# The last products of two token blocks made together: two levels of Strassen's scheme in place of one, with the outer sums of the weights made in DRAM

## The chip, the core and the metric

The kernel runs on one core of one Trainium2 chip. The metric is the device time of one execution in microseconds; lower is better.

## The reference

The reference is one decoder layer on `x`, 1024 tokens (2 sequences of 512) of 1024 features, all in float32. Three parts follow each other, and after each the input of the part is added and a layer norm is taken:

```python
# 1 attention over features: per token, q is [32, 32 heads], k and v are [32, 8 heads] repeated 4 times
scores = einsum('bsdh,bseh->bsde', q, k) / sqrt(32)
out    = einsum('bsde,bseh->bsdh', softmax(scores), v)
# 2 product with the context, both sides rounded to 8 bits
matmul(fake_quant(x, 8/255, 128), fake_quant(ctx, 8/255, 128))
# 3 feed-forward with a routed part
h      = relu(x @ up_w) ** 2                            # 1024 -> 2048
routed = (x @ fc1_w) @ expert_w * sum(top2(x @ gate_w))  # 1024 -> 512 -> 512
layernorm(h @ down_w + routed @ fc2_w) * gamma + beta
```

Part 1 has no product between tokens: it is elementwise work of 32 x 32 sums for each token. Part 3 holds most of the arithmetic. Its last step is a product of 2560 features (2048 of `h`, 512 of the routed part) with 2560 x 1024 weights.

## The kernel before

Tokens lie in eight tiles of 128, and two tiles make a block, so there are four blocks. The text calls a tile "a token" where it says token 2, token 3 and so on, as the code's names do (`s_3`, `xc_4`).

The work has two tracks. **The tokens' path** (`token_path`, L636) takes the tiles one after another. `scores` (L428) multiplies q and k on DVE (L435) and sums over heads (L441) in four pieces. `exponentials` (L448) takes the row maximum (L450) and subtracts it (L451) on DVE, and then takes exp on ACT (L454). `attend` (L458) multiplies with v (L468), sums (L474), divides (L479) and adds to the residual `xc` (L489). `normalise_aside` (L309) makes the layer norm: ACT makes the sum (L317), the squares (L322), the variance (L324), POOL the power (L326), ACT the shift (L330) and the result (L331). `cross` (L575) rounds on ACT (L346, L349, L352, L602), transposes with a DMA from ACT's queue (L605), multiplies with the rounded context on PE (L618) and adds to `xc` on DVE (L611, L612, L623). `hand_over` (L683) transposes the tile for the feed-forward (L133, L134) and adds the last norm's beta with an accumulating DMA from POOL's queue (L690). `context_beside` (L510) rounds the second sequence's context beside all this.

**The feed-forward** is PE's track. For blocks 0 and 1 `ffn` (L768) makes 16 products of 128 hidden features (L780, 8 chunks of weights of 1 MB, two PSUM banks `ps_mm` in turn), each taken out by ACT's relu (L798) and square (L799), then 4 products of the routed part taken out by DVE (L809), and then `down` (L983), the last product over 20 pieces of 128 features, accumulated in four PSUM banks (L994). `gate_of` (L723) makes the routing. For blocks 2 and 3 `ffn_pair` (L824) makes the first products of both together by Strassen's scheme in ten steps of 7 products (L881), and then `down_seven` (L1039) makes the last product of one block and then of the other: for each half of the 1024 columns and each group of four pieces, `weight_sums` (L1027) loads 1 MB and makes four sums of weights on DVE, `unit_sums` (L1014) makes four sums of hidden features, and 7 x 2 matmuls of 128 x 128 by 128 x 256 follow (L1080). In all these are 2 blocks x 2 halves x 5 groups x 14 = 280. Seven products stand for the eight of a 2 x 2 product of blocks.

A front stage comes first: queries, keys and values of all eight tiles are made on PE (`project_qk`, `project_v`), those of tiles 2 to 7 go through staging tiles (`new_qkv`, L167) into `qkv_d` in DRAM with accumulating DMAs (`projected`, L179), and `fetch_qkv` (L173) brings them back one tile ahead of their scores from POOL's queue. `expert_w` and `fc2_w` are multiplied there into `e2`, 512 x 1024 in DRAM, so that the routed part has one product fewer later.

The program is written as generators that interleave both tracks. The loop at the end of the kernel advances the tokens' path while the sum of its yielded weights times PACE = 0.7 is below the sum of the feed-forward's. A scheduler then orders each engine's instructions by its own estimates, except where `tc.issue_after` pins one instruction behind another. On the chip each engine takes its queue strictly in that order and waits on semaphores for what it needs. A pool that is opened after another was closed takes over its memory; whoever first writes there waits for the last use of what lay there, DMAs included.

## Time and profile before

| | us |
|---|---|
| median of 3 runs (lowest to highest) | 727.29 (725.45 to 727.51) |
| profiled execution | 725.26 |
| its span in the profile | 723.2 |
| outside the span | 2.06 |
| front stage, to the first scores of token 2 | 0 to 139.4 |
| block 0, to the first of block 1's products | 139.4 to 309.9 |
| block 1, to the pair's first product | 309.9 to 466.2 |
| pair, first products | 466.2 to 588.6 |
| pair, last products | 588.6 to 709.6 |
| tail | 709.6 to 723.2 |

Times in a timeline or a window count from the start of the span. A row of a timeline has the start, the busy time, engine, line and operation, what is written and read, and in brackets how long the engine stood idle before and what ended that. Rows of groups have the busy time, the mean of one in ns, and the idle time before them. The trace counts a float32 matmul as two rows, so 560 rows of L1080 are 280 products of the program.

### The profile page before, as it was taken

To read this page: it belongs to the slowest core of one execution; us is meant where nothing else is said; L and a number is where in the kernel's file an instruction comes from. 1 tells how busy PE (TensorE), PEld (TensorE's weight loads), DVE (VectorE), ACT (ScalarE), POOL (GpSimd) and SP (SyncE) were. 2 spreads that over 40 slices of the span, in tenths; PEclk is the share of its full clock that TensorE was granted. 3 is DMA by queue.
4 is the path that set the end of the run, shared out by engine and by line. 5 is a ranking of instruction groups with operands and counts; after the bars stand their busy time and mean duration, and the time that the engine had idled before them with its cause. 6 is when DMAs were issued, how large, how long until landed. Compare 5 with 4: busy or idle time off the path is not lost. (4 is left out here: it accounts for less than half of the span.)

```text
span 723.2 us, 7274 instructions
## 1 busy us (share of the span) xinstructions
PE 696.0 (96%) x2802; PEld 494.5 (68%) x2812; DVE 545.3 (75%) x619; ACT 239.1 (33%) x389; POOL 63.8 (9%) x96
## 2 busy tenths in 40 slices
PE   6999998999999999999999999999999999999992
PEld 3656653468876444478785444588888888888882
DVE  4799987599999999999899920545545754779736
ACT  2097643222644389138453141212422100000001
POOL 2011211210001020011010000100100000001001
PEclk9999999999999999999999999999999999999996
DMA  8999523695455666456448344522332235556501
GB/s 284 340 296 374 155 39 102 216 293 165 154 163 157 203 230 203 150 162 229 131 147 218 116 157 149 155 78 77 127 105 100 61 116 176 174 174 205 201 1 58
DMA packets 71554, 120.05 MB, mean 166 GB/s; under 512 B 10640, under 2 KB 44944, under 8 KB 71520
## 3 DMA queue, kind: packets, MB, share of 16 engines
q1 hardware_dynamic: 57344, 98.84, 40.4%
q0 software_dynamic: 6496, 18.39, 9.9%
q10 hardware_dynamic: 7680, 2.36, 1.5%
q8 instruction: 22, 0.36, 0.2%
q14 instruction: 12, 0.10, 0.0%
HBM read 106.73 MB, written 11.01 MB: 163 GB/s over the span
## 5 line engine op out<-in xcount | busy, mean ns | idle before, releaser
L994 PE MATMUL pd<-dn,h 128*128 128x512 f32 x320 | 138.7, 592 | 0.0
L780 PE MATMUL pu<-x2T,up 128*128 128x256 f32 x512 | 112.4, 380 | 1.3 <-DMA up<-in_L_ffn_up_w_dram 0.8
L994 PEld LDWEIGHTS pd<-dn,h 128*128 128x128 f32 x320 | 60.5, 190 | 73.2 <-issue 72.7
L780 PEld LDWEIGHTS pu<-x2T,up 128*128 128x128 f32 x512 | 96.8, 190 | 15.6 <-ACT relu L798 1.2
L435 DVE TENSOR_TENSOR pqk<-qk 128x2048 f32<-128x2048 f32 x32 | 72.4, 2282 | 0.0
L441 DVE TENSOR_REDUCE s<-pqk 128x256 f32<-128x2048 f32 x32 | 72.3, 2277 | 0.1
L468 DVE TENSOR_TENSOR pav<-s,v 128x2048 f32<-128x2048 f32 x32 | 72.2, 2277 | 0.0
L474 DVE TENSOR_REDUCE o<-pav 128x64 f32<-128x2048 f32 x32 | 71.9, 2266 | 0.0
L152 PE MATMUL pqk<-wqkv,xT 128*128 128x512 f32 x128 | 66.1, 616 | 0.8 <-DVE wqkv L233 0.5
L1034 DVE TENSOR_TENSOR tt<-dn 128x1024 f32<-128x1024 f32 x20 | 24.3, 1221 | 24.7 <-DMA dn<-in_L_ffn_down_w_dram 15.5
L157 PEld LDWEIGHTS pv<-wqkv,xT 128*128 128x128 f32 x128 | 24.3, 190 | 24.2 <-issue 22.0
L1080 PE MATMUL ps<-dn,h 128*128 128x256 f32 x160 | 40.4, 379 | 0.0
L1080 PE MATMUL ps<-dn,s 128*128 128x256 f32 x160 | 40.4, 379 | 0.0
L1080 PE MATMUL ps<-tt,h 128*128 128x256 f32 x160 | 40.4, 379 | 0.0
L1092 ACT COPY y<-ps 128x256 f32<-128x256 f32 x4 | 1.5, 372 | 109.9 <-PE ps L1080 109.9
L157 PE MATMUL pv<-wqkv,xT 128*128 128x256 f32 x128 | 35.6, 379 | 0.0
L1080 PEld LDWEIGHTS ps<-dn,s 128*128 128x128 f32 x160 | 30.4, 190 | 4.1
L1080 PEld LDWEIGHTS ps<-tt,h 128*128 128x128 f32 x160 | 30.4, 190 | 4.1
L1080 PEld LDWEIGHTS ps<-dn,h 128*128 128x128 f32 x160 | 30.4, 190 | 4.1
L152 PEld LDWEIGHTS pqk<-wqkv,xT 128*128 128x128 f32 x128 | 24.3, 196 | 12.6 <-issue 5.5
L419 PE MATMUL pe<-fc,exT 128*128 128x512 f32 x64 | 29.9, 619 | 2.5 <-DVE xc L623 2.5
L326 POOL TENSOR_TENSOR rstd<-ve,neg_half 128x1 f32<-128x1 f32 x18 | 14.1, 784 | 200.9 <-ACT ve L324 200.2
(204 smaller groups left out, 1009.5 us busy)
## 6 DMA issues: line engine op xcount, KB each, us to landing
dn<-in_L_ffn_down_w_dram SPq DMA_DIRECT2D x32, 1024.0 KB, 5.1
up<-in_L_ffn_up_w_dram SPq DMA_DIRECT2D x16, 1024.0 KB, 5.5
dn<-e SPq DMA_DIRECT2D x8, 1024.0 KB, 5.0
pair<-in_L_ffn_up_w_dram SPq DMA_DIRECT2D x8, 1024.0 KB, 5.3
fc<-in_L_ffn_fc_w_dram SPq DMA_DIRECT2D x6, 1024.0 KB, 5.9
xs<-in_x_dram SPq DMA_DIRECT2D x8, 512.0 KB, 7.4
wq<-in_L_attn_Wq_dram SPq DMA_DIRECT2D x8, 512.0 KB, 6.1
xc<-in_x_dram SPq DMA_DIRECT2D x8, 512.0 KB, 8.4
```

The costliest lines, as they stand in the source:

```text
L152: projecting[0] = nc.tensor.matmul(pqk, xT[:, k, :], wqkv[k][:, 0 : 2 * DG], start=(k == 0), stop=(k == KE - 1))
L157: nc.tensor.matmul(pv[:, :DG], xT[:, k, :], wqkv[k][:, 2 * DG : 3 * DG], start=(k == 0), stop=(k == KE - 1),)
L326: nc.gpsimd.tensor_tensor(rstd, ve, neg_half, ALU.pow)
L419: expert[0] = nc.tensor.matmul(ps, exT[:, m, ts(l, P)], fc2[m // 2][:, m % 2, ts(n, HALF)], start=(m == 0), stop=(m == NL - 1),)
L435: nc.vector.tensor_tensor(prod.rearrange("p (d e g) -> p d e g", d=DC, g=G), q3[:, ts(c, DC), :].unsqueeze(2).to_broadcast([P, DC, D, G]), ...
L441: nc.vector.tensor_reduce(s[:, ts(c, DC), :].rearrange("p d e -> p (d e)"), prod.rearrange("p (c g) -> p c g", g=G), AX.X, ALU.add,)
L468: nc.vector.tensor_tensor(prod.rearrange("p (d g e) -> p d g e", d=DC, g=G), s[:, ts(c, DC), :].unsqueeze(2).to_broadcast([P, DC, G, D]), ...
L474: nc.vector.tensor_reduce(o[:, ts(c, DC), :].rearrange("p d g -> p (d g)"), prod.rearrange("p (c e) -> p c e", e=D), AX.X, ALU.add,)
L780: lately[0] = nc.tensor.matmul(ps[:, :NB], ws[:, k, wcols], xT[:, k, :], start=(k == 0), stop=(k == KE - 1))
L994: lately[0] = nc.tensor.matmul(pd[i][n], h[kk // 4][:, i, kk % 4, :], w[:, k, ts(n, HALF)], start=(kk == 0), stop=(kk == NK - 1),)
L1034: nc.vector.tensor_tensor(tt[:, 0:2], w[:, 1], w[:, :, 0], ALU.subtract)
L1080: began[m] = lately[0] = nc.tensor.matmul(banks[m], units[jj][m][:, k, :], weights[gg][m][:, k, :], start=begins and not second, stop=(jj ...
```

## The change

Four things are changed.

1. The last products of blocks 2 and 3 are made together by Strassen's scheme on two levels. The outer level splits the two blocks (rows), the halves of each group's 512 features and the halves of the columns; each of its seven products is made by an inner level of seven. There are 49 x 5 matmuls of 128 x 128 by 128 x 256, 245.
2. The outer level's sums of weights don't depend on tokens. `outer_sums` makes them in DRAM: for four of the seven (`OUTER_T`) and each of three chunks of groups, a copy from SP's queue and an accumulating DMA from POOL's queue, each over DRAM alone, 1 MB for the first two chunks and 0.5 MB for the last. They are issued a step at a time beside blocks 0 and 1.
3. `new_h` makes one tile per block instead of five, and the sums of hidden features get tiles of a pool `units` and of `late`. Pool `more` is closed before the pair.
4. The staging tiles of queries, keys and values move from `attp` (where their tags were shared with the sums of hidden features) to `frontp`, which is closed before pools `h`, `ffn`, `sums` and `more` are opened.

The core of the diff:

```diff
     qkv_d = scratch.tile([NT, P, 3 * DG], F32, name="qkv_d")
-    KEPT = NK // 4
+    KEPT = 5
 
     def new_qkv(t, away):
-        pool, bufs = (attp, KEPT) if away else (tokp, 2)
-        qk = pool.tile([P, 2 * DG], F32, tag="s12" if away else "qk", name=f"qk_{t}", bufs=bufs)
-        v = pool.tile([P, G, D], F32, tag="s4" if away else "v", name=f"v_{t}", bufs=bufs)
+        pool, bufs = (frontp, KEPT) if away else (tokp, 2)
+        qk = pool.tile([P, 2 * DG], F32, tag="qk", name=f"qk_{t}", bufs=bufs)
+        v = pool.tile([P, G, D], F32, tag="v", name=f"v_{t}", bufs=bufs)
         return qk, v
 
...
-    def new_h(blk, k):
+    def new_h(blk):
 
         pool, tag = (pools["late"], "h_late") if blk > PAIR else (pools["h"], "h")
-        return pool.tile([P, TB, 4, P], F32, tag=tag, name=f"h_{blk}_{k}", bufs=NK // 4)
+        return pool.tile([P, NG, TB, 4, P], F32, tag=tag, name=f"h_{blk}")
...
-        h = ([], [])
-        sums = []
+        h = [new_h(blk) for blk in blks]
+        outer_steps, outer = outer_units(*h)
+        down = down_pair(outer)
+        next(down)
...
+            if g % 2 == 1:
+                next(outer_steps)
+                if g // 2 + 1 in [hi for _, hi in CHUNKS]:
+                    next(down)
         phase[0] = "down"
-        down_seven(PAIR, h[0], sums, next_block)
-        down_seven(PAIR + 1, h[1], next_sums)
+        next(down, None)
...
-        if blk < PAIR:
+        if blk < NBLK - 1:
             sums = small.tile([P, 1], F32, tag="sum3", name=f"sum3_{blk}_{i}")
             nc.vector.scalar_tensor_tensor(
                 y, y, rstd, xcs_of[blk][i], ALU.mult, ALU.add, accum_out=sums
             )
-            later.append(store_aside(rows, y, sums, f"3_{blk}_{i}", len(later)))
+            aside = store_aside(rows, y, sums, f"3_{blk}_{i}", len(later))
+            if blk < PAIR:
+                later.append(aside)
+            else:
+                for _ in aside:
+                    pass
             return
         nc.vector.scalar_tensor_tensor(y, y, rstd, xcs_of[blk][i], ALU.mult, ALU.add)
-        if blk < NBLK - 1:
-            normalise(y, f"3_{blk}_{i}")
-            nc.gpsimd.dma_start(rows, y)
-            return
 
...
+    CHUNKS = ((0, 2), (2, 4), (4, 5))
 
...
+    OUTER_T = (4, 5, 6, 7)
+    tw = {
+        (m, c): scratch.tile([(hi - lo) * 2 * P, HALF], F32, name=f"tw_{m}_{c}")
+        for m in OUTER_T for c, (lo, hi) in enumerate(CHUNKS)
+    }
+
+    def raw_rows(c, half, n):
+
+        lo, hi = CHUNKS[c]
+        src = down_w if 4 * lo < NI else e2
+        lo, hi = (lo, hi) if 4 * lo < NI else (lo - NI // 4, hi - NI // 4)
+        v = src.rearrange("(j h q) n -> j h q n", h=2, q=2 * P)
+        return v[lo:hi, half, :, ts(n, HALF)]
+
+    def outer_sums():
+
+        for _ in range(12):
+            yield
+        for c, (lo, hi) in enumerate(CHUNKS):
+            b11, b12, b21, b22 = (raw_rows(c, half, n) for half in range(2) for n in range(2))
+            t = {m: tw[m, c].rearrange("(j q) n -> j q n", q=2 * P) for m in OUTER_T}
+            for to, src in ((5, b11), (7, b12), (6, b22), (4, b21)):
+                nc.sync.dma_start(t[to], src)
+                for _ in range(2):
+                    yield
+            for to, src in ((5, b12), (7, b22), (6, t[5]), (4, t[6])):
+                nc.gpsimd.dma_start(t[to], src, accum_op=ALU.add, max_dma_last_dim=4 * HALF)
+                for _ in range(6):
+                    yield
+
+    def outer_units(ha, hb):
+
+        ss = [
+            pools[pool].tile([P, NG, TB, 2, P], F32, tag=f"units_{i}", name=f"units_{i}")
+            for i, pool in enumerate(("units", "units", "late"))
         ]
+        a11, a12, a21, a22 = (h[:, :, :, 2 * k : 2 * k + 2, :] for h in (ha, hb) for k in range(2))
+
+        def steps():
+            for j in range(NG):
+                s1, s2, s4 = (s[:, j] for s in ss)
+                nc.vector.tensor_tensor(s1, a21[:, j], a22[:, j], ALU.subtract)
+                nc.vector.tensor_tensor(s2, s1, a11[:, j], ALU.subtract)
+                nc.vector.tensor_tensor(a21[:, j], a11[:, j], a21[:, j], ALU.subtract)
+                nc.vector.tensor_tensor(s4, a12[:, j], s2, ALU.add)
+                yield
+
+        return steps(), {1: a11, 2: a12, 3: ss[2], 4: a22, 5: ss[0], 6: ss[1], 7: a21}
+
+
+    OUTER = ((1, 0), (5, 1), (6, 0), (7, 1), (3, 0), (2, 1), (4, 0))
+
+    def down_pair(outer):
+        inner_units, inner_weights = {}, {}
+
+        def units_of(o, lo=0, hi=NG):
+
+            m = OUTER[o][0]
+            x = outer[m]
+            a11, a12, a21, a22 = (x[:, :, i, k, :] for i in range(2) for k in range(2))
...
+        def weights_of(o, c):
+
+            m = OUTER[o][0]
+            lo, hi = CHUNKS[c]
+            nj = hi - lo
+            tag = ("wb", "wb", "wa", "wa")[len(inner_weights) % 4]
+            w = wstream.tile([P, nj, 4, QW], F32, tag=tag, name=f"dn_{m}_{c}")
+            if m in OUTER_T:
+                src = tw[m, c].rearrange("(j k r) n -> r j k n", k=2, r=P)
+            else:
+                src = raw_rows(c, int(m != 1), int(m == 3))
+                src = src.rearrange("j (k r) n -> r j k n", r=P)
+            to = w.rearrange("p j (k e) n -> p j k (e n)", k=2)
+            if m in OUTER_T:
+                nc.sync.dma_start(to, src)
+            else:
+                for j in range(nj):
+                    nc.sync.dma_start(to[:, j], src[:, j])
+            tt = pools["sums"].tile([P, 3, nj, QW], F32, tag="tt", name=f"tt_{m}_{c}")
+
+            b12 = w[:, :, 1, :]
+            t1, t3, t4 = tt[:, 0], tt[:, 1], tt[:, 2]
+            nc.vector.tensor_tensor(
+                tt[:, 0:2], w[:, :, 0::3, :].rearrange("p j q n -> p q j n"),
+                b12.unsqueeze(1).to_broadcast([P, 2, nj, QW]), ALU.add,
+            )
+            nc.vector.tensor_tensor(b12, w[:, :, 3, :], t1, ALU.add)
+            nc.vector.tensor_tensor(t4, w[:, :, 2, :], b12, ALU.add)
+            inner_weights[o, c] = {
+                1: w[:, :, 0, :], 2: w[:, :, 2, :], 3: w[:, :, 3, :], 4: t4, 5: t1, 6: b12, 7: t3
+            }
+
...
+            for mm in (1, 6, 7, 5, 4, 2, 3):
+                for cc in range(c, c + along):
+                    lo, hi = CHUNKS[cc]
+                    for j in range(lo, hi):
+                        with tc.issue_after(lately[0].ins):
+                            lately[0] = nc.tensor.matmul(
+                                banks[mm], unit(o, mm, j),
+                                inner_weights[o, cc][mm][:, j - lo, :],
+                                start=(j == 0 and mm not in FIRST_OF),
+                                stop=(j == NG - 1 and mm not in FIRST_OF.values()),
                             )
+            i += along
...
+            if m == 6:
+
+                nc.gpsimd.dma_start(c12, c11, accum_op=ALU.add)
+            elif m == 3:
+                nc.gpsimd.dma_start(to, p5, accum_op=ALU.add)
+
+                def rest(to=to):
+                    nc.vector.tensor_tensor(c12, to, c12, ALU.subtract)
+                    for t in range(TB):
+                        measure(0, 1, t)
+
+            elif m == 7:
+
+                nc.gpsimd.dma_start(c21, c12, accum_op=ALU.add)
+
+                def rest():
+                    nc.vector.tensor_tensor(c22, p5, c21, ALU.subtract)
+                    for t in range(TB):
+                        measure(1, 1, t)
+
...
-    pools["h"] = ctx.enter_context(tc.tile_pool(name="h", bufs=NK // 4))
+    pools["h"] = ctx.enter_context(tc.tile_pool(name="h", bufs=1))
 
     pools["ffn"] = ctx.enter_context(tc.tile_pool(name="ffn", bufs=2))
     pools["sums"] = ctx.enter_context(tc.tile_pool(name="sums", bufs=3))
-    pools["more"] = ctx.enter_context(tc.tile_pool(name="more", bufs=1))
+    first_blocks = ExitStack()
+    pools["more"] = first_blocks.enter_context(tc.tile_pool(name="more", bufs=1))
+    adding = outer_sums()
+    later.append(adding)
...
+    for _ in adding:
+        pass
     tokens_only.close()
+    first_blocks.close()
+    pools["units"] = ctx.enter_context(tc.tile_pool(name="units", bufs=1, reuse_waits="tile"))
     pools["late"] = ctx.enter_context(
         tc.tile_pool(name="late", bufs=1, side="right", reuse_waits="tile")
     )
```

Of the seven outer products (`OUTER`: which product, and which of two sets of PSUM banks), every one is taken out of PSUM by ACT's copy and sums on DVE as in `down_seven`, into halves of two tiles `y_a` and `y_b`; three of the outer level's sums of results are accumulating DMAs from POOL's queue between tiles (as `c12` plus `c11` above). `outer_units` takes four sums of hidden features per group beside the pair's first products, and `units_of` four more for each outer product beside the outer product before it. Block 2's ending, which went over DVE and POOL, now goes over ACT (`store_aside`).

## The prediction

> **What bounds the kernel now.** I read the page's busy shares and costliest groups first, then the busy times by stage, then the timelines of ACT, DVE and POOL where the tokens' path runs beside the products.
>
> ```profile
> PE 696.0 (96%) x2802; PEld 494.5 (68%) x2812; DVE 545.3 (75%) x619; ACT 239.1 (33%) x389; POOL 63.8 (9%) x96
> L780 PE MATMUL pu<-x2T,up 128*128 128x256 f32 x512 | 112.4, 380 | 1.3 <-DMA up<-in_L_ffn_up_w_dram 0.8
> L1080 PE MATMUL ps<-dn,h 128*128 128x256 f32 x160 | 40.4, 379 | 0.0
> ```
>
> PE is busy for 96% of the span and hardly waits. By stage (time; PE, PEld, DVE, ACT, POOL busy; granted clock; DMA share; GB/s):
>
> ```profile
> 0.00:139.40 139.40, 129.23 (x449) 73.81 (x453) 108.24 (x101) 64.98 (x90) 24.62 (x40) 0.99 0.72 226
> 139.40:309.90 170.50, 168.17 (x629) 105.69 (x631) 167.00 (x121) 80.13 (x123) 15.01 (x23) 1.00 0.61 192
> 309.90:466.20 156.30, 155.14 (x595) 100.95 (x598) 115.39 (x112) 61.82 (x118) 12.87 (x18) 1.00 0.51 160
> 466.20:588.60 122.40, 122.40 (x575) 107.75 (x573) 66.73 (x137) 28.41 (x51) 3.42 (x5) 1.00 0.31 96
> 588.60:709.60 121.00, 121.00 (x561) 106.27 (x559) 80.78 (x138) 1.49 (x4) 5.88 (x7) 1.00 0.43 148
> 709.60:723.20 13.60, 0.04 (x1) 0.00 (x0) 7.15 (x17) 2.33 (x3) 2.01 (x3) 0.58 0.21 77
> ```
>
> The reader is to see that in block 0 (second row) DVE is as full as PE, 167.0 against 168.2 of 170.5: the tokens' scores and sums are a second full track, and the two only fit because neither waits for the other. In the fifth row PE alone works. The third view, ACT's timeline, shows where the tracks touch: one queue serves both, relu (L798) for PE and exp (L454) for DVE.
>
> ```profile
> 155.78 0.38 ACT L798 ACTIVATE relu<-pu 128x256 f32<-128x256 f32 x1 [3.25 <-PE pu L780]
> ...
> 159.59 1.06 ACT L454 ACTIVATE s<-s 128x1024 f32<-128x1024 f32 x1
> ...
> 203.04 1.06 ACT L454 ACTIVATE s<-s 128x1024 f32<-128x1024 f32 x1
> ...
> 247.71 1.06 ACT L454 ACTIVATE s<-s 128x1024 f32<-128x1024 f32 x1 [6.72 <-DVE s L451]
> ```
>
> These are block 0's first relu and the exponentials of tokens 2, 3 and 4. DVE's timeline shows what the last waits for, and how far apart tokens are:
>
> ```profile
> 158.34 1.22 DVE L451 TENSOR_TENSOR s<-s,smax 128x1024 f32<-128x1024 f32 x1
> ...
> 185.97 1.21 DVE L489 SCALAR_TENSOR_TENSOR xc<-xc,o 128x1024 f32<-128x1024 f32 x1
> ...
> 201.79 1.22 DVE L451 TENSOR_TENSOR s<-s,smax 128x1024 f32<-128x1024 f32 x1
> ...
> 246.45 1.22 DVE L451 TENSOR_TENSOR s<-s,smax 128x1024 f32<-128x1024 f32 x1
> ```
>
> **The part that saves.** L1080 has 560 rows in 121.0 us, two rows to a product: 280 products of 0.432. After, 49 × 5 = 245: 35 × 0.432 = −15.1, stage 105.9. Its feeding fits: an outer product has 15.1 us of PE beside some 11 to 13 of DVE (by the distance of starts in runs of like instructions: 1.13 for 1024 wide, 0.60 for 512, 0.33 for 256; unit sums of 640 an estimated 0.73 between them) and 2.5 MB of loads (the dn rows: 1 MB in 5.1). The three accumulates between tiles on POOL's queue are nearest to the 512 KB row of 7.3 and have most of an outer product, 15.1, before their sum is read: nothing, and up to 4 on DVE, not PE, without it. I add 0.4 for the last outer product, bounds 0 and 3. In the tail the last combinations queue behind DVE's row order: from PE's end to the last shift 7.97 now, about 10.9 then: +2.9, bounds +0.6 (DVE free) and +5.
>
> **The part that moves.** The projections' staging tiles go from attp to frontp. The pools opened after frontp closes (h, relu, sums) lie over them, so block 0's first relu gets waits for the staging's accumulate DMAs. These have landed long before 155 us and cost nothing by themselves (cover: they are issued before 140, rows of 4.8 and 6.3 us). But the order of the program as built changes with them. On ACT's queue the exponentials of tokens 2, 3 and 4 now stand ahead of block 0's first relu (before: the relu ahead of all three), and token 5's ahead of the fifth chunk's first relu. On DVE's queue tokens 2 to 5 come ahead of token 2's cross attention. PE's ps_mm has two banks: after two up products it waits for a relu.
>
> First stall. A token's turn on DVE is 41.8: 8 pairs for scores and 8 for sums at 2 × 2.2 each (two products a pair of rows, 35.2), max and subtraction 2.4, den 1.2, rden 0.3, division 0.3, L489 1.1, exp 1.1. Token 2's subtraction ends at 159.6 as now, token 3's at 201.4, token 4's at 242 (token 3's L489 stands behind it, −1.1). Exp 1.06, relu 0.38: PE restarts at 243.7 where it ran on at 160.0: **+83.7**.
>
> Second stall. PE makes eight products (3.45 each) to 271.4, then needs the relu behind token 5's exp. That turn contains token 3's L489, whose xc load stands on SP behind up chunk 3, and so behind PE's 250.7. Landing rows of that load are 3.3, 8.4 (median) and 14.0: I take about 7, so DVE waits 9 (from 249; bounds 4 and 14). Subtraction at 292.7, PE at 294.6: **+23.2**; 0.4 of routing products comes off (earlier now). Delay 106.5.
>
> Then token 2's layer norm is late: ACT gets to it after 295, and POOL's rstd for it stands behind the fetch of token 7's qk (which waits for token 5's scores) and three accumulates.
>
> ```profile
> 189.23 0.59 POOL L326 TENSOR_TENSOR rstd<-ve,neg_half 128x1 f32<-128x1 f32 x1 [11.47 <-ACT ve L324]
> 198.48 0.58 POOL L175 DMA_DIRECT2D qk<-qkv_d  x1 [8.66 <-DVE pqk L435]
> ```
>
> In POOL's timeline of before, rstd is ahead of the fetch. ACT's passes (about 1.2 each, six of them), transpose (5.0) and PE's row order then give these PE waits, each by summing the same rows onward: aT of token 2 1.2, of token 3 5.6, the context row behind ACT's passes 7.0, the gate behind L623 5.4 (19.2, less 0.8 of such waits now): **+18.4**, and block 1 starts at 434.8 instead of 309.9. In block 1, ACT's asides ahead of a relu: 6.0 (less 1.0 now): **+5.0**. Between blocks 1 and 3 the crosses of tokens 6 and 7 stand after all of block 1's last products instead of inside them: 6.8, 7.2, 4.3, 1.5: **+19.8**. Each of these five groups has 0 as its lower bound, if the DVE and ACT work behind it has caught up.
>
> **The weights summed in DRAM.** 12 copies on SP and 12 accumulates on POOL, 10 MB each. q1 has 98.84 MB in 40.4% of the span (3.0 us per MB), q0 18.39 in 9.9% (3.9): 10 × 3.0 + 10 × 3.9 = 69 us of the engines' time in 430 us of blocks 0 and 1, whose shares are 0.61 and 0.51 unstretched. I take 0 on PE; the cover is that up chunks land in 5.5 and are used for 6.9, so PE loses only what a load takes beyond 6.9. The first copy stands ahead of up chunk 0 on SP and may put it back by its own 5, which the first stall covers; without that stall it would be 5. An accumulate is nearest to the 512 KB row of xc and ln_beta, 7.3, so 1 MB may take 15: if each of POOL's chains of accumulates held an rstd that long, +15 at most.
>
> **Restarting PE.** After waiting 4.1 at the start, eight transposes take 1.94 instead of 1.04, though the granted clock reads 1.00 there: 0 to 0.9 per wait of over 4 us, of which there are eight: 0 to 7. I take 0, since restarts into a chain that ACT or DVE sets are hidden. The clock does fall when PE idles: 0.58 in the last row. The Trainium skill, "TensorE: Matmul & The Clock Gate", "What's actually happening", goes further: half rate after an idle window of about 3.4 us until about 3.4 us of work. By it each such wait would cost an estimated 1.7, together 14, and the sum would end at 877; no row here has a restart in mid-kernel.
>
> **Sum.** 83.7 + 23.2 − 0.4 + 18.4 + 5.0 + 19.8 = 149.7 late into the last products; −15.1 + 0.4 + 2.9. 723.2 + 149.7 − 11.8 = 861.1; 2.06 lies outside the span: 863.2. The profiled run (725.26) is 2.0 below the median of 727.29, so 865.
>
> **Rivals.** (1) The order doesn't bind: then only the end changes, 727.3 − 11.8 = 715.5, faster. It decides if ACT reaches block 0's first relu at about 156, that is, if the exponentials of tokens 3 and 4 are not in fact ahead of it. For it: PE-bound rows everywhere. Against: one queue runs in order, and the order as built is plain. 0.04. (2) The two stalls stay but the later waits are absorbed: 865 − 18.4 − 5.0 − 19.8 = 822, and 817 with the load at its lower bound. For it: PE has some 380 us of work left at 314 and DVE only two tokens' scores. Up to 840: 0.22. (3) Copies, accumulates and restarts cost their upper ends: 865 + 15 + 7 + 5 (load) = 892 and a little more: 880 to 905, 0.14. For it: DMA shares are already 0.5 to 0.6. (4) The sums in DRAM or the smaller scheme don't save: the last stage stays at 121, 880; inside (3)'s range.
>
> **How the numbers follow.** The likeliest (840 to 880) has 0.58, the rest 0.02. 820 to 890 leaves out a tenth of (2), half of (3) and all of (1). A difference of 0.3% (2.2 us) is about what this kernel's runs can tell. Faster 0.04, within 0.3% 0.01, slower 0.95.
>
> **What would show it.** Right: ACT's exponentials at about 160, 202 and 242 with no relu between; PE idle from about 159 to 244 and 271 to 295; rstd of token 2 near 297; block 1's first product near 435; pair up 121 to 123 long without waits; 245 products in about 106; 11 from PE's end to the last shift. Wrong: a relu at 156; PE waits for up loads of several us each; PE waiting for tt or units in the last stage; a span that ends before 815.

## The result, and the profile after

The changed kernel takes **992.52 us** (median of 4 runs, 987.93 to 993.52) beside 726.94 of the kernel before on the same chip: ratio 1.3645, 95% interval 1.3596 to 1.3694. The forecast was 865, at most 890. The sign was right, and 138 of the 266 us of loss were named; the rest was not seen.

The stages by the same marks as before (front, block 0 in six pieces, block 1, pair's first products, last products, tail); columns: time; PE, PEld, DVE, ACT, POOL busy; granted clock; DMA share; GB/s:

```profile
0.00:139.80 139.80, 129.92 (x452) 73.81 (x453) 108.61 (x101) 64.85 (x90) 24.46 (x40) 0.99 0.72 218
139.80:243.50 103.70, 20.34 (x87) 12.20 (x85) 100.54 (x61) 7.20 (x12) 7.77 (x9) 0.61 0.21 62
243.50:320.00 76.50, 25.92 (x97) 21.48 (x97) 46.28 (x27) 6.92 (x16) 5.28 (x4) 0.63 0.39 95
320.00:367.80 47.80, 30.72 (x115) 25.26 (x116) 1.44 (x2) 12.85 (x25) 1.60 (x2) 0.82 0.72 143
367.80:435.60 67.80, 48.94 (x162) 30.14 (x161) 44.80 (x33) 20.90 (x31) 5.69 (x5) 0.88 0.65 160
435.60:517.60 82.00, 32.30 (x81) 14.17 (x81) 1.68 (x5) 27.72 (x35) 8.85 (x10) 0.71 0.78 163
517.60:556.40 38.80, 33.53 (x97) 14.19 (x97) 31.02 (x28) 5.54 (x8) 1.59 (x2) 0.86 0.37 91
556.40:723.70 167.30, 151.75 (x542) 98.94 (x543) 55.56 (x68) 50.04 (x101) 11.75 (x17) 0.98 0.61 182
723.70:862.60 138.90, 131.69 (x630) 112.34 (x629) 78.75 (x157) 39.03 (x68) 5.84 (x9) 0.98 0.28 82
862.60:973.60 111.00, 106.43 (x486) 92.85 (x485) 89.20 (x145) 6.76 (x15) 5.93 (x7) 0.98 0.52 156
973.60:991.60 18.00, 1.50 (x7) 0.96 (x6) 12.94 (x27) 4.73 (x8) 3.46 (x6) 0.64 0.30 117
```

Block 0 now lasts from 139.8 to 556.4: 416.6 us where it took 170.5. That is 246 of the 268 us by which the span grew. In its worst piece (435.6 to 517.6) PE is idle for 50 of 82 us and DVE for 80, while the DMA share is 0.78: the loads are late. ACT's timeline shows the first part of it, and the page's group for the relu's wait its price:

```profile
159.64 1.06 ACT L454 ACTIVATE s<-s 128x1024 f32<-128x1024 f32 x1 [6.72 <-DVE s L451]
201.34 1.06 ACT L454 ACTIVATE s<-s 128x1024 f32<-128x1024 f32 x1 [40.64 <-DVE s L451]
242.08 1.06 ACT L454 ACTIVATE s<-s 128x1024 f32<-128x1024 f32 x1 [39.68 <-DVE s L451]
243.05 0.37 ACT L796 ACTIVATE relu<-pu 128x256 f32<-128x256 f32 x1
```

The three exponentials stand ahead of the relu at the predicted times (159.6, 201.4, 242), and PE restarts at 243.47 (predicted 243.7). The forecast parts from the profile after that. The list of PE's waits (total, times, longest):

```profile
PE pu L780 <- ACT relu L796: 85.2, 2, 82.9
PE pu L780 <- DMA up<-in_L_ffn_up_w_dram: 67.7, 5, 39.5
PE pd L984 <- DMA dn<-in_L_ffn_down_w_dram: 45.1, 1, 45.1
PE py L618 <- DMA aT<-a: 18.6, 3, 14.7
PE pt_x L134 <- ACT xc L331: 14.2, 3, 5.4
```

Loads of up and dn chunks hold PE for 112.8 us, where the forecast had none, and the transposing DMA of the tokens' path (aT) for 18.6, where it had 6.8. DVE has the like: its L489 waits 101.9 us in five waits for `xc<-in_x_dram`, of which I had counted one of 9. The list of DMA issues gives the median time to landing, in the last column (the first line is of the kernel before, the others of the changed kernel):

```profile
up<-in_L_ffn_up_w_dram SPq DMA_DIRECT2D x16, 1024.0 KB, 5.5
...
up<-in_L_ffn_up_w_dram SPq DMA_DIRECT2D x16, 1024.0 KB, 22.3
dn<-in_L_ffn_down_w_dram SPq DMA_DIRECT2D x16, 1024.0 KB, 9.4
xc<-in_x_dram SPq DMA_DIRECT2D x8, 512.0 KB, 20.2
tw<-in_L_ffn_down_w_dram POOLq DMA_DIRECT2D x4, 1024.0 KB, 58.1
```

An up chunk took 5.5 before and takes 22.3; the accumulate of 1 MB into `tw`, which I had put at 15 at most, takes 58.1. Yet the DMA engines are not full. These are two windows of the same kernel while the accumulate that POOL issued at 238.10 is in flight (it lands after 59.1, and the next, issued at 297.43, after 57.1):

```profile
276.00:284.00 8.00, 4.40 (x21) 3.53 (x19) 8.00 (x5) 1.60 (x4) 0.00 (x0) 0.90 0.14 33
284.00:292.00 8.00, 0.00 (x0) 0.00 (x0) 8.00 (x5) 0.00 (x0) 0.00 (x0) 0.50 0.14 34
```

A share of 0.14 is two of 16 engines (0.125) and a little. On SP a copy of the same kind was issued at 254.08, and behind it, at 259.94, an up chunk that takes 59.8 to land; PE needs it from 280 on and gets it at 319.9. The rest of the time goes to a slower PE: the same products as in the run *spread* below, but 713.0 us busy against 683.4 (2742 and 2732 records; a few are missing in both), while the granted clock reads 0.50 to 0.71 in the stretches with long waits. The difference between the two spans, 271.2, is so split into idle time (278.6 against 37.0) and busy time (29.6). Two rows of the changed kernel's PE timeline, each of 16 up products, show both:

```profile
319.91 8.85 PE L780 MATMUL pu<-x2T,up 128*128 128x256 f32 x32 [39.52 <-DMA up<-in_L_ffn_up_w_dram]
...
616.89 7.07 PE L780 MATMUL pu<-x2T,up 128*128 128x256 f32 x32
```

### The profile page after: what moved, and what is told of

It is laid out like the page before. It is cut to its first block, busy times and chain, and to the rows that moved or that the text cites. A ratio compares the mean times of both kernels' runs of the same rounds, so it can differ in the third digit from the quotient of the medians.

```text
span 991.6 us, 7279 instructions
## 1 busy us (share of the span) xinstructions
PE 713.0 (72%) x2742; PEld 496.3 (50%) x2742; DVE 570.8 (58%) x649; ACT 246.5 (25%) x404; POOL 82.2 (8%) x111
## 2 busy tenths in 40 slices
DMA packets 95923, 140.09 MB, mean 141 GB/s; under 512 B 25408, under 2 KB 59712, under 8 KB 95888
## 5 line engine op out<-in xcount | busy, mean ns | idle before, releaser
L780 PE MATMUL pu<-x2T,up 128*128 128x256 f32 x512 | 125.5, 408 | 155.8 <-ACT relu L796 85.2
L780 PEld LDWEIGHTS pu<-x2T,up 128*128 128x128 f32 x512 | 104.8, 207 | 175.3 <-ACT relu L796 86.0
L489 DVE SCALAR_TENSOR_TENSOR xc<-xc,o 128x1024 f32<-128x1024 f32 x7 | 8.6, 1225 | 101.9 <-DMA xc<-in_x_dram 101.9
L618 PE MATMUL py<-cq,aT 128*128 128x512 bf16 x128 | 30.9, 397 | 18.6 <-DMA aT<-a 18.6
L454 ACT ACTIVATE s<-s 128x1024 f32<-128x1024 f32 x8 | 8.4, 1056 | 135.2 <-DVE s L451 135.2
L796 ACT ACTIVATE relu<-pu 128x256 f32<-128x256 f32 x32 | 12.2, 381 | 106.6 <-PE pu L780 105.0
L780 PE MATMUL pl<-x2T,fc 128*128 128x256 f32 x128 | 31.4, 408 | 8.6 <-DMA fc<-in_L_ffn_fc_w_dram 8.6
L346 ACT ACTIVATE ctx<-ctx,z,rs 128x1024 f32<-128x1024 f32 x16 | 19.5, 1238 | 60.2 <-DMA ctx<-in_ctx_dram 60.2
L623 DVE SCALAR_TENSOR_TENSOR xc<-py,ns,xc 128x512 f32<-128x512 f32 x16 | 11.8, 745 | 37.5 <-PE py L618 37.4
L780 PEld LDWEIGHTS pl<-x2T,fc 128*128 128x128 f32 x128 | 26.1, 206 | 14.1 <-issue 8.1
## 6 DMA issues: line engine op xcount, KB each, us to landing
up<-in_L_ffn_up_w_dram SPq DMA_DIRECT2D x16, 1024.0 KB, 22.3
```

Of the source, the lines that this page charges most:

```text
L346: nc.scalar.activation(tmp, src, AF.Relu, scale=rs, bias=z)
L618: crossed[t] = nc.tensor.matmul(py, aT[:, k, :], cq[:, k, ts(h, HALF)], start=(k == 0), stop=(k == KC - 1))
L780: lately[0] = nc.tensor.matmul(ps[:, :NB], ws[:, k, wcols], xT[:, k, :], start=(k == 0), stop=(k == KE - 1))
L796: nc.scalar.activation(r, ps, AF.Relu)
```

## The experiments

Times are medians. Ratios and intervals are to the kernel before. A run without an interval has one time.

| run | what differs | us | ratio |
|---|---|---|---|
| changed kernel | | 992.52 | 1.3645 [1.3596, 1.3694] |
| tile | waits for reused memory by tile | 993.47 | |
| wide | `tw` transfers with rows outermost | 771.24 | 1.0632 [1.0587, 1.0678] |
| c1n | wide, first copy as in the change | 847.54 | |
| a1n | wide, first accumulate as in the change | 803.01 | |
| cw_an | wide copies, all accumulates as in the change | 955.87 | |
| doses | wide, four accumulates with slowest dimension 2 to 16 | 815.72 | |
| nosum | outer sums left out | 722.84 | 0.9978 [0.9936, 1.002] |
| paced | wide, copies behind weight loads | 789.82 | 1.0866 [1.0799, 1.0933] |
| paced3 | wide, accumulates too | 762.61 | 1.0464 [1.0387, 1.0542] |
| pairtime0 | wide, sums beside the pair's first products | 751.91 | 1.0323 [1.027, 1.0376] |
| pairtime | the same, other order at the end | 752.13 | 1.0313 [1.0263, 1.0363] |
| spread | wide, one accumulate per step | 724.31 | 0.9973 [0.9937, 1.0008] |

**Is it the staging move?** The forecast laid the new order to memory: relu's tiles lie over the staging tiles and wait for them. *tile* takes that wait away, so that a tile waits only for what lay in its own place:

```diff
-    pools["h"] = ctx.enter_context(tc.tile_pool(name="h", bufs=1))
+    pools["h"] = ctx.enter_context(tc.tile_pool(name="h", bufs=1, reuse_waits="tile"))
-    pools["ffn"] = ctx.enter_context(tc.tile_pool(name="ffn", bufs=2))
+    pools["ffn"] = ctx.enter_context(tc.tile_pool(name="ffn", bufs=2, reuse_waits="tile"))
```

> The changed kernel with pools h and ffn waiting by tile instead of by pool, so that block 0's first relu no longer waits for the staging tiles' accumulates. The prediction on record named these waits as what changed the order. If so and they matter: the first stall goes, 880 to 910. Theory W: they are innocent, the order as built is the same as in the changed kernel: 980 to 1000.

The time is 993.47, PE's wait for the relu 85.9, and the exponentials stand as they did (160.04, 201.74, 242.47, then the relu at 243.43). That cause is false. *nosum*, further down, also has the staging tiles where the change put them, and there the relu (156.83) stands ahead of the exponentials (160.56).

**Is it the shape of the transfers?** In the change the source of a sum is a view of two groups, 256 rows and 512 columns (`j q n`, in steps of 524288, 1024 and 1): its slowest dimension is 2. *wide* only turns the view; the same bytes go to the same places:

```diff
-            t = {m: tw[m, c].rearrange("(j q) n -> j q n", q=2 * P) for m in OUTER_T}
+            t = {m: tw[m, c].rearrange("(j q) n -> q j n", q=2 * P) for m in OUTER_T}
+            b11, b12, b21, b22 = (b.rearrange("j q n -> q j n") for b in (b11, b12, b21, b22))
```

> The copies and accumulates of outer_sums get the 256 rows of a half group as their outermost dimension instead of the two groups; the bytes and the sums are the same. As built, block 0's first relu then stands ahead of the exponentials of tokens 3 and 4 again. Theory W (few engines): the two-group form runs on few DMA engines, is slow itself (58.1 us for 1 MB) and holds up every load that needs all engines; and the order of the queues came from the scheduler's estimate of these same transfers. It expects accumulates of 10 to 20 us, up chunks landing in 5 to 8 instead of 22.3, PE waits for loads under 15 in all, and 712 to 735 in total. Theory V (volume): the 20 MB of extra traffic hold up the loads; order repaired, but up chunks still over 15, total 830 to 900. Theory O (the order alone, as on record): the 83 us stall and what follows it go, the waits for loads (67.7 for up and 45.1 for dn chunks) stay: 850 to 880.

771.24: 221 of the 266 us go, not all that the theory of few engines expected (712 to 735); what is left is taken up further down. Two lines from ACT's timeline and the list of issues of *wide*:

```profile
196.03 0.38 ACT L796 ACTIVATE relu<-pu 128x256 f32<-128x256 f32 x1 [3.25 <-PE pu L780]
...
199.76 1.05 ACT L454 ACTIVATE s<-s 128x1024 f32<-128x1024 f32 x1
```

```profile
up<-in_L_ffn_up_w_dram SPq DMA_DIRECT2D x16, 1024.0 KB, 5.3
tw<-in_L_ffn_down_w_dram POOLq DMA_DIRECT2D x4, 1024.0 KB, 22.9
```

The relu is ahead of the exponentials again, up chunks land in 5.3, and the accumulate in 22.9 (expected 10 to 20). So one shape carries both losses, the order and the late loads. *c1n* and *a1n* give the old shape back to one transfer each, the first copy or the first accumulate, and *cw_an* to all accumulates:

```diff
+            spread = lambda v: v.rearrange("j q n -> q j n")
...
 # c1n: copies
+                turn = spread if (c, at) != (0, 0) else (lambda v: v)
+                nc.sync.dma_start(turn(t[to]), turn(src))
 # a1n: accumulates
+                turn = spread if (c, at) != (0, 0) else (lambda v: v)
+                nc.gpsimd.dma_start(turn(t[to]), turn(src), accum_op=ALU.add, max_dma_last_dim=4 * HALF)
 # cw_an: accumulates
+                turn = spread if False else (lambda v: v)
```

> As the run with wide transfers, but the very first copy keeps the two-group form; as built, the exponentials of tokens 2, 3 and 4 stand ahead of block 0's first relu again, as in the changed kernel, and token 5's behind the fifth chunk's relu. This isolates the order of the queues with one slow transfer. Theory W: first stall of 83 as in the changed kernel, no second stall, loads fast; 84 over the wide run and up to 43 of later waits: 800 to 845. Theory V: over 900. If the order were harmless: as the wide run.

> As the run with wide transfers, but the very first accumulate keeps the two-group form; as built, the first relu stands ahead of the exponentials of tokens 3 and 4. This isolates one slow transfer without the order. Theory W: it takes about 58 us, up chunks that fly beside it land in about 22 instead of 6 and PE uses one per 6.9, so PE loses up to 58 x (1 - 6.9/22.3) = 40: 20 to 40 over the wide run. Theories V and O: within 5 of the wide run.

> As the run with wide transfers, but all accumulates keep the form of the changed kernel: of them four from the inputs are two-group, 1 MB each. The first relu stands ahead of the exponentials of tokens 3 and 4. Theory W: four times the loss of the run with one, 80 to 160 over the wide run. Theories V and O: within 10 of the wide run.

*c1n*: 847.54 (expected 800 to 845), 76 over *wide*, and the wait for the relu is back whole:

```profile
PE pu L780 <- ACT relu L796: 82.9, 1, 82.9
PE pu L780 <- DMA up<-in_L_ffn_up_w_dram: 30.5, 3, 23.1
```

One copy in the old shape is enough for the bad order. So the layout of the program answers to the shape of the copies on SP; that it does so by an estimated duration of the transfer is my reading, not shown. *a1n*: 803.01, 32 over *wide*, with the good order; its one slow accumulate takes 68.6 to land. The expectation of 20 to 40 was met, but not by the path that it named, up chunks that come late: PE waits 6.0 for those, as in *wide* (5.9). PE's two large waits are these:

```profile
PE pe L419 <- ACT e L423: 47.8, 1, 47.8
PE py L618 <- DMA aT<-a: 25.4, 1, 25.4
```

In the first, ACT's shift (L330) waits 49.84 for an rstd that runs on POOL only at 194.66, behind a fetch that waited 39.5 for the slow accumulate and seven more accumulates issued after it. *cw_an*: 955.87, 185 over *wide* (expected 80 to 160), also with the good order; the accumulates take 59.2, and PE's largest sum of waits is for the transposing DMA, `aT<-a`: 102.8 in six, against 15.8 for up chunks. So a slow accumulate costs by whatever the tokens' path needs next of the DMA engines or of POOL's queue, not by weights alone. The parts (76 and 185) are more than the 221 together, so they overlap: PE can't wait for a load while it waits for the relu.

**Few engines or small packets?** The old shape also comes with more small packets: those under 512 B are 25408 in the changed kernel and 11184 in *wide*. *doses* cuts the four accumulates from the inputs into halves of 512 KB with a slowest dimension of 2, 4, 8 and 16 rows:

```diff
-                nc.gpsimd.dma_start(t[to], src, accum_op=ALU.add, max_dma_last_dim=4 * HALF)
+                rows = {(0, 5): 2, (0, 7): 4, (1, 5): 8, (1, 7): 16}.get((c, to))
+                ...
+                    for g in range(2):
+                        part = [v[:, g].rearrange("(b a) n -> a b n", a=rows) for v in (t[to], src)]
+                        nc.gpsimd.dma_start(*part, accum_op=ALU.add, max_dma_last_dim=4 * HALF)
```

> The four accumulates from the input weights are cut into halves of 512 KB each, and the slowest dimension of the access pattern of each pair of halves is 2, 4, 8 and 16 rows, in this order; nothing else of the wide form is changed. If the slowest dimension sets how many of the 16 DMA engines work on a transfer, a half lands in about 29 us at 2 (half of the 58.1 of the changed kernel), 15 at 4, 8 to 12 at 8 and 16 (where other traffic, not the engines, sets the time: the wide form took 22.9 for a whole MB). While only the halves at 2 are in flight the DMA share is about 0.13. If it was the row-by-row cutting of the two-group form (packets under 512 B: 25408 against 11184 in the wide form), all four doses take alike.

Landing: 40.1 and 31.4 at 2; 17.0 and 29.1 at 4; 17.1 and 18.0 at 8; 11.0 and 6.3 at 16. The first at 2, the second at 4 and both at 8 are longer than I expected; the doses also follow each other in time, and other transfers are beside most of them. The windows say more. Here are four of *doses*, each inside the flight of a half, with 2, 4, 8 and 16 in this order:

```profile
141.00:146.00 5.00, 5.00 (x13) 2.15 (x12) 0.82 (x3) 2.42 (x6) 1.18 (x2) 1.00 0.14 26
208.00:212.00 4.00, 0.00 (x0) 0.00 (x0) 4.00 (x3) 0.00 (x0) 0.00 (x0) 0.50 0.27 69
264.00:266.00 2.00, 0.00 (x0) 0.00 (x0) 0.00 (x0) 2.00 (x3) 0.00 (x0) 0.50 0.54 154
337.00:341.00 4.00, 4.00 (x17) 1.95 (x16) 4.00 (x5) 1.20 (x2) 0.00 (x0) 1.00 0.90 126
```

The share is 0.14, 0.27, 0.54 and 0.90: 2, 4, 8 and most of 16 engines. The packets don't tell against it. By the sizes kept in the traces the extra ones have 8 bytes each, 14336 in the changed kernel, 5632 in *doses* (512 rows × (7 + 3 + 1)) and none in *wide*, while POOL's queue has the same 6416 packets of 2048 B in all three: the rows are not cut. Nor are small packets under way where the time goes. These are the packets of the changed kernel from 262 to 300, of all queues and then of POOL's (packets, MB, share):

```profile
DMA packets 656, 1.29 MB, mean 34 GB/s; under 512 B 6, under 2 KB 84, under 8 KB 655
q0 software_dynamic: 287, 0.58, 8.3%
```

The starts and durations of the packets also tell how many are under way at once, those of POOL's and of SP's queue together: from 262 to 297 two for 80% of the time and three for the rest, in *doses* two or three at a dose of 2 (141 to 145), never fewer than four at 4 and eight at 8 (exactly four for 68% and exactly eight for 41% of the two windows). The trace doesn't name a packet's engine; that the others stood idle is inferred from this and from the share. In 208 to 212 the two up chunks issued from 193.8 on are still unfinished: they land after 20 us and more, and the share stays at 0.27 until 214, past the half's landing at 212.2. I read this as a load that spreads over all engines waiting for its part on the few that the accumulate holds; by this reading two busy engines are enough to delay it. The Trainium skill, "DMA: Bandwidth & Descriptors", "Why a DMA increments its semaphore by 16 and not by 1", has the rule: the number of engines is the largest one up to 16 that divides the slowest dimension, leaving out those of size 1, of both sides. The four shares above agree with it.

**What is the scheme itself worth?** *nosum* leaves the outer sums of weights out and multiplies with raw rows of the weights (its output is therefore not the layer's); all else is as in the change.

```diff
-            if m in OUTER_T:
-                src = tw[m, c].rearrange("(j k r) n -> r j k n", k=2, r=P)
-            else:
-                src = raw_rows(c, int(m != 1), int(m == 3))
-                src = src.rearrange("j (k r) n -> r j k n", r=P)
+            src = raw_rows(c, int(m != 1), int(m == 3))
+            src = src.rearrange("j (k r) n -> r j k n", r=P)
...
-    adding = outer_sums()
-    later.append(adding)
+    adding = iter(())
```

> Leaves out the sums of weights in DRAM: the four outer products that need them use raw rows of the weights, loaded like the other three, so the output is not the layer's. All else is as in the changed kernel, the staging tiles in frontp too. As built, the first relu stands ahead of the exponentials of tokens 3 and 4. Theory W and V: the sums alone made the loss, 716 to 724, PE's last stage 105 to 111. If the moved staging tiles or the single tile for h cost something: over 730.

722.84, ratio 0.9978: not told apart from the kernel before. The stages to 466.2 are as they were, so moving the staging tiles and making one tile of `h` cost nothing. The last products go from 590.29 to 704.45, 114.2 where they took 121.0: 6.8 saved, not 14.7. DVE is busy 89.16 of the 111.40 us up to 700, PE waits 4.9 for its sums of weights (L1115), and it is slow after that. Two rows of *nosum*'s PE timeline, five products (ten rows) each:

```profile
691.19 4.47 PE L1179 MATMUL ps<-tt,h 128*128 128x256 f32 x10
...
697.82 2.32 PE L1179 MATMUL ps<-tt,h 128*128 128x256 f32 x10
```

The first follows a wait of 3.24 and takes 4.47 in place of 2.32. From PE's end to the end of the span 16.45 pass instead of 13.6.

**Can the sums be hidden?** *wide* still loses 44 us. Its front stage is at a DMA share of 1.01, and there POOL's queue stops: an accumulate that reads another's result waits for its landing, and a layer norm's rstd stands behind it. Rows of POOL and ACT of *wide*:

```profile
116.18 1.52 POOL L1033 DMA_DIRECT2D tw<-tw  x1 [18.15 <-DMA tw<-tw]
...
119.11 2.58 POOL L326 TENSOR_TENSOR rstd<-ve,neg_half 128x1 f32<-128x1 f32 x1
```

```profile
121.72 0.29 ACT L330 ACTIVATE shift<-rstd,parts 128x1 f32<-128x1 f32 x1 [38.05 <-POOL rstd L326]
```

In the kernel before, that rstd ran at 84.3. PE then waits 29.9 for ACT. Four placements were tried to get out of this: *paced* issues each copy on SP behind the last weight load, *paced3* also spreads the accumulates, each behind the last rstd, and in the last stage takes the sum that waits for the accumulate between tiles one chunk later, *pairtime0* moves copies and accumulates beside the pair's first products, and *pairtime* also changes the order of the last outer product.

```diff
 # paced
+                with tc.issue_after(loaded[0].ins):
+                    nc.sync.dma_start(t[to], src)
 # paced3, pairtime0 and pairtime, also
+            with tc.issue_after(powed[0].ins):
+                nc.gpsimd.dma_start(t[m], src, accum_op=ALU.add, max_dma_last_dim=4 * HALF)
 # pairtime0 and pairtime, in the pair's loop of first products
+            for _ in range(3):
+                next(adding, None)
 # pairtime
-            for mm in (1, 6, 7, 5, 4, 2, 3):
+            for mm in (1, 6, 7, 5, 4, 2, 3) if along == 1 else (1, 2, 3, 6, 7, 5, 4):
```

> As the run with wide transfers, and each copy is pinned on SP's queue behind the weight load issued last before it, so that the copies can't go ahead into the front stage. Theory W with the front stage crowded out: the 30.3 of PE waits for xT in the front stage and the 5.9 for an up chunk go, block 0's first up product is back at about 153: 715 to 735, where the upper half is for POOL's accumulates standing ahead of token 2's rstd. Theory V (volume): the waits move to blocks 0 and 1, total still 750 or more.

> As the run with pinned copies; besides, the accumulates are spread over blocks 0 and 1 by kind, with their copies at least one kind ahead, and pinned on POOL's queue behind the rstd issued last; and in the last stage the sum that waits for the accumulate between tiles is taken one chunk later. Theory W: no wait of over 2 us for loads or rstds in blocks 0 and 1, the 4.9 of PE waits in the last outer product shrink: 711 to 720. Theory V: 745 or more. If the end of the kernel gives back what the 35 products save: 722 to 730.

> The same with the last outer product's inner products in their old order 1, 6, 7, 5, 4, 2, 3. Expected 5 to 8 above the run with the new order, that is 720 to 726; if the PE waits in the last outer product cost nothing, the same as that run within 2.

> As the run with wide transfers, but the copies and accumulates are issued beside the pair's first products, a few per step, pinned behind the pair's weight loads; and the last outer product makes its inner products in the order 1, 2, 3, 6, 7, 5, 4, so that the three that need only raw weights come first. In that stage the DMA share was 0.31 and POOL had 3 us of work in the kernel before. If what the wide sums still cost (48 over the run without sums) comes from standing beside the loads of the front stage and ahead of the rstds of blocks 0 and 1: block 1 starts at about 310 and the pair at about 467, and the total is that of the run without sums, 722.8, less the 4.9 of PE waits and some 3.4 of slow matmuls after them in the last outer product, plus 1 or 2 in the tail: 713 to 720. If the volume itself costs: pair loads late, 728 or more.

All four missed: 789.82, 762.61, 751.91, 752.13. *paced* moves the copies out of the front stage, and PE then waits 20.9 us for ACT's xc up to 307.9, where ACT itself has stood 18.3 for a context load (22.7 to landing, issued from POOL's queue right behind two accumulates), and 17.8 for up chunks, the longest 11.4. In *paced3* aT lands in 8.4 and PE waits 20.7 for it, in three waits. In *pairtime0* both blocks are as before, and the pair's loads are crowded out instead: share 0.99 from 466.2 to 588.6, and 28.7 us of waits for them. The other order in *pairtime* takes PE's wait at the end from 4.0 to 1.3 and the time doesn't move; that DVE's work sets that end fits this, but no run shows it.

*spread* puts no two accumulates close together: the copies ride on SP beside the last products of blocks 0 and 1, and each step of the pair's first products issues one accumulate, behind a one-column operation on POOL that reads that step's `h`:

```diff
+            tick = small.tile([P, 1], F32, tag="tick", name=f"tick_{g}")
+            powed[0] = nc.gpsimd.tensor_tensor(tick, h[0][:, g // 2, 0, 2 * (g % 2), 0:1], neg_half, ALU.mult)
+            next(adding)
...
+            if 2 <= c < 8:
+                next(adding)
```

> The outer sums in the wide form, spread thin: the 12 copies ride on SP beside blocks 0's and 1's last products, and one accumulate is issued at each step of the pair's up products (the last two behind the first outer products), so that no two of them are in flight together for long. If what the earlier placements lost was only the crowding of 1 MB accumulates (DMA share 0.98 to 0.99 in 466 to 588 us where all of them were issued there together), PE then waits for no load of the pair for more than 2 us in total, and the time is that of the kernel without outer sums, 722.8, and a little for the copies: 722 to 732. If the volume itself costs wherever it is put (the pair's own loads already take 0.31 of the DMA engines in that stage, and the accumulates add some 72 us of engine time to 122 us), the sum is above 745, with PE waiting for up and dn chunks between the steps. Against the kernel before (726.9) neither gives more than 0.5% gain.

724.31 (720.81 to 729.95), ratio 0.9973 [0.9937, 1.0008], within 1.5 us of *nosum*, which is less than the runs of either differ among themselves. Issues and the pair's window of *spread*:

```profile
tw<-in_L_ffn_down_w_dram POOLq DMA_DIRECT2D x4, 1024.0 KB, 10.5
tw<-tw POOLq DMA_DIRECT2D x4, 1024.0 KB, 9.4
...
466.20:588.60 122.40, 122.40 (x598) 107.06 (x597) 74.57 (x147) 29.90 (x54) 18.89 (x25) 1.00 0.74 163
```

PE is busy for all of the 122.4 us, at a DMA share of 0.74; *pairtime0* had the twelve copies in this stretch as well, at 0.99, and PE busy for 93.7. Over the whole kernel the volume is the same, and it is hidden when it is thin enough. This is the best version found, and it is no faster than the kernel before: what the scheme saves on PE is 6.8 less 2.9 in the tail less 1.7 ahead of the last products (590.29 against 588.60).

## Why the prediction was wrong, step by step

**Right.** The first stall (83.7; measured 82.87), its place, and that ACT's one queue makes it: the relu behind three exponentials. Why they stand so was wrong (below), so its size came out on a cause that was not the real one. A token's turn on DVE, 41.8 (measured 41.70 from exponential to exponential); it has eight rows for scores and eight for sums at 2.2, which is the 35.2 of the sum, not eight pairs of each. 245 products. The tail's +2.9 (16.45 − 13.6 in *nosum*). That the accumulates would hold an rstd on POOL's queue: the mechanism of *wide*'s 29.9 us and of *a1n*'s 47.8, priced at 15 at most.

**The step that failed** is "The weights summed in DRAM … I take 0 on PE", with "1 MB may take 15" and "+15 at most". I priced the transfers by their bytes and by the rows of other DMAs on the same queue, and did not look at the shape. Measured: 58.1 us for 1 MB, at a share of two engines of 16, and up chunks of 22.3 instead of 5.5. With the order as good as before (*cw_an*) the four accumulates alone cost 185 us. The condition that I gave for this ("PE loses only what a load takes beyond 6.9") fits the changed kernel, where up and dn chunks hold PE for 112.8, with an input that was wrong; it left out the transposing DMA and POOL's queue, which carry most of *cw_an* and *a1n*. The 69 us of engine time were only one side: averaged over 16 engines, they hid a few engines that were full.

**The cause of the order** ("the order of the program as built changes with" the staging tiles) was wrong in its cause and right in its effect: *tile* leaves the order as it is, *wide* restores it. The first stall is also a consequence of the DMA shape.

**Second stall and what follows.** I had PE back at 294.6 with relu as the releaser. It was back at 270.98 after 11.07 for an up load, and then waited 39.52 for the next. The xc load that "I take about 7" took 20.2 to land, and DVE's wait of 9 was one of 24.63. Block 1 began at 556.4, not 434.8: 122 of the 127 us that the forecast was short. Rival 1 needed the relu at 156; it stands at 243. Rival 2, that later waits are absorbed, finds no support; rival 4 was half right (6.8 of 14.7 saved); rival 3 named the right transfers, at a price some twelve times too small (15 against the 185 of *cw_an*).

**Restarting PE.** "I take 0", bounds 0 and 7 for eight waits of over 4 us: measured 29.6, of which 20.5 is in the up, fc and dn products (13.1, 3.2 and 4.2), whose records are complete. There are twelve such waits after 139, and *spread* has none. I called restarts hidden because another engine sets the chain; where a load sets it, PE's slow products delay all that comes after. One restart can be read: 32 rows of up products take 8.78 to 9.42 after waits of 4.9 to 39.5, and 7.07 without, so 1.7 to 2.4 more. The page's rule that the prediction cites and sets aside (half rate after an idle window) agrees with the trace: the granted clock is 0.50 from 284 to 292 and from 298 to 319, where PE stands. Its estimated 1.7 per wait would make 20 here.

**Last products.** 105.9 + 0.4 was forecast; 112.4 in the changed kernel (862.66 to 975.09). PE waits 4.6 for DVE's sums of weights, longest 3.2: "0.4, bounds 0 and 3" was for a track that I had taken as having 2 to 4 us to spare in every outer product; in the last, it has none.

## What to carry to other kernels

Before costing a DMA by its bytes, write down its access pattern and look at the slowest dimension on both sides: two there made a 1 MB accumulate land in 58.1 us where 10.5 were possible, and loads beside it came late, while the mean DMA share said that all was quiet. A share that stands still at a simple fraction of 16 while something waits for a load is the sign of it in a profile. When work is hidden beside other work, spread it one transfer at a time: the same 24 transfers cost 29 to 67 us over *nosum* in clumps and, spread out, 1.5, which can't be told from nothing.

## What the runs showed that I had not expected

- An accumulate between DRAM tensors took 58.1 us per MB with a slowest dimension of 2, 22.9 with 256 in a stage at a DMA share of 1.01, and 10.5 with 256 when one was issued per step, at 0.74.
- Small loads suffer as well: in the changed kernel a fetch of 128 KB (v from qkv_d, issued at 299.04) took 56.0 us to land beside the accumulate issued at 297.43.
- The shape of one copy (*c1n*) changes where ACT's relu stands in the program, for 76 us.
- The extra small packets of the old shape (8 bytes each) looked like rows cut up, but the row packets of 2048 B are the same in number.
- Five products (ten rows) after a wait of 3.24 us took 4.47 instead of 2.32, at the end of *nosum*, whose clock reads 0.97 in that stage and 0.99 to 1.00 in those before.
